# A two-layer relational graph convolution on one core: 123 single-row tiles in place of 116, spread by other steps over two DMA-issuing engines

## The chip, the cores and the metric

The kernel runs on one core of one Trainium2 chip. A core has five engines with an instruction queue each: PE (TensorE, matrix products), DVE (VectorE), ACT (ScalarE), POOL (GpSimd) and SP (SyncE). DMAs are started by SP, ACT and POOL, and the queue of an engine is worked off in order. The metric is the device time of one execution in microseconds. The profile holds one execution, with its own time.

## The reference

Two layers of a relational graph convolution over 12500 nodes with 128 features and 200000 edges of 8 relations, then a residual and a layer norm. Edges come sorted by destination. Cut to what is computed:

```python
def _rgcn_conv(x, src, dst, et, basis, comp, root, bias):
    W = jnp.einsum('rb,bio->rio', comp, basis)
    xw = jnp.einsum('ni,rio->nro', x, W)
    msgs = xw[src, et]
    seg = dst * N_REL + et
    summed = jax.ops.segment_sum(msgs, seg, num_segments=N_NODES * N_REL)
    cnt = jax.ops.segment_sum(jnp.ones(...), seg, num_segments=N_NODES * N_REL)
    mean = summed / jnp.maximum(cnt, 1.0)[:, None]
    agg = mean.reshape(N_NODES, N_REL, HIDDEN).sum(axis=1)
    return agg + x @ root + bias
...
h = x
for l in range(2):
    h = jax.nn.relu(_rgcn_conv(h, src, dst, et, basis[l], comp[l], root[l], bias[l])) + h
return _layernorm(x + h)
```

## The kernel before

The 200000 edges are 1563 tiles of 128 edges, and eight tiles make an octet: 196 octets (Q = 8, NQ = 196). Each layer is one pass over the octets. The order of the instructions on every engine is written out by hand in `ordered_path`: calls of `plan.add` record an operation with the cells it reads and writes, and `plan.emit` writes them out with the semaphore waits that follow from those cells. Nothing is scheduled by a tool, so what stands behind what in an engine's queue is the order of these calls.

*Gathers.* Per tile, POOL issues one indirect DMA that fetches 128 rows of 512 bytes (`gather`, L766): in layer 1 rows of `x`, in layer 2 rows of `y_d`, a table in DRAM of every node's features times every relation's weights, 51 MB. They land in `rows`, a ring of seven octets, and are issued five octets ahead (AHEAD = 5). The last six octets (LATE = 6, from octet 190) are different: they are issued two octets ahead in the program's order (CLOSE = 2), and each has one more wait, for the latest octet of means then in the order. So gather(190) waits until PE has done octet 187, gather(191) octet 188, and so on. The gathers of layer 2 stand behind all gathers of layer 1 in POOL's queue, and one of them (L760, with a fix-up list) waits for the whole table to have been stored.

*Single-row tiles.* For some tiles POOL issues nothing. Instead SP or ACT loads the offsets of the rows into registers (L697) and starts one DMA of 512 bytes per row (L702). `lists` names these tiles: an engine, a first tile, an end, a step, the rows that one operation fetches (a part), the lead in octets, and the places where rows land. The places are buffers that are free at that time: `jmp`, `comp_sb` and `sel` for SP in layer 1; five quarters of a `y_row` buffer, then two of `mixer`, for ACT in layer 1; the two `sT` buffers in layer 2. `lone_rows` hands the parts out in each octet: for SP all parts whose tile is within the lead, for ACT one part per octet of each list. Before, layer 1 has 32 such tiles on SP (in parts of 32 rows), and 5 and 18 on ACT (in parts of 16, eight octets for a tile); layer 2 has 31 on SP and 30 on ACT, in parts of 32. That is 55 + 61 = 116, and POOL's gathers are 1508 and 1502.

*Layer 1.* In octet o of the loop come, in this order: `gathers`; `means(o)`, PE's products of the rows with the weighted one-hots of their destinations (L1276); a batch of copies on ACT (L623: a half of the table `y_row`, the product `ys` and two halves of `sT`) with the store of a table block to `y_d` (L620), if one is complete; the parts on SP; the one-hots of octet o + 2 on DVE (L1188); the part on ACT; `product(o - 1)` on PE (L1308), which needs the `sT` that ACT copied; `place(o - 2)` (L1339); and up to two halves of a table block on PE (L1406). PE's next octet of means writes the banks that ACT's copies read. From octet 53 to octet 187 each octet has an ACT part.

*Layer 2.* In octet q come: `gathers`, the parts on SP and on ACT, `add_rows` on PE (L1451), the one-hots of octet q + 2 on DVE, and one step of a list `todo`. A finished group of eight node tiles puts ten steps on it: transposes, an addition, statistics, `aggr` (L1530), a square root on ACT (`root_of`, L1533), two empty ones, a reciprocal on DVE (`one_by`, L1537), the scaling and the store. For the last full group the transposes come at octet 178, the root at 182 and the reciprocal at 185.

The last lines of the layer 1 loop that bear on this:

```python
        means(o)
        batch(o)
        ...
        if o > 1:
            lone_rows(0, "SP", o)
        ...
        onehot(0, o + 2, o - 1)
        ...
        if o > 1:
            lone_rows(0, "ACT", o)
        ...
            product(o - 1)
```

Of the kernel before, what the change touches and what calls it, by code (L numbers as in the profile page):

```python
# [8 lines left out]
F32 = mybir.dt.float32  # L9
# [419 lines left out]
def ordered_path(  # L429
# [26 lines left out]
    P = 128  # L456
# [11 lines left out]
    Q = 8  # L468
# [29 lines left out]
    def keep(shape, dtype, name):  # L498
        return const.tile(shape, dtype, name=name)
# [16 lines left out]
    jmp = keep([P, P], I32, "jmp")  # L516
# [37 lines left out]
    comp_sb = keep([P, L * R * NB], F32, "comp_sb")  # L554
# [8 lines left out]
    mixer = keep([P, L * R, K], F32, "mixer")  # L563
# [39 lines left out]
    plan = Plan(tc, {"hw": 8, "aq": 4, "gq": 4, "sr": 8, "ar": 8})  # L603
# [35 lines left out]
    def floats(t, n):  # L639
        return t[:, n * P:(n + 1) * P]  # L640

    sT_f = [t.rearrange("p r g k -> p (r g k)") for t in sT_r.tiles]
    yr_f = yr_r.tiles[0].rearrange("p r d -> p (r d)")
    yr_cells = [("y_row", 0, 0), ("y_row", 0, 1)]
    mixer_f = mixer.rearrange("p m k -> p (m k)")
    idx_f = idx.bitcast(F32)
    lists = [
        [("SP", 90, 1552, 47, 32, 15, [(jmp.bitcast(F32), ["jmp"], []), (comp_sb, ["comp"], []),
                                     (sel.rearrange("p g k -> p (g k)"), ["sel"], [])]),
         ("ACT", 13 * Q + 2, 46 * Q, 8 * Q, 16, 10, [(floats(yr_f, j), yr_cells, yr_cells) for j in range(5)]),  # L650
         ("ACT", 53 * Q + 2, 1552, 8 * Q, 16, 10, [(floats(mixer_f, j), ["mixer"], []) for j in range(2)])],
        [("SP", 62, 1552, 49, 32, 15, [(floats(sT_f[0], j), [("sT", 0, 0), ("sT", 0, 1)], []) for j in range(4)]),
         ("ACT", 65, 1552, 50, 32, 15, [(floats(sT_f[1], j), [("sT", 1, 0), ("sT", 1, 1)], []) for j in range(4)])]]
    single, at_row = [{}, {}], [0, 0]
    for l in range(L):
        for k, (_, t0, t1, by, _, _, hosts) in enumerate(lists[l]):
            for i, t in enumerate(range(t0, t1, by)):
# [4 lines left out]
    offs = iota_f.bitcast(I32)  # L662
    byte = mybir.dt.uint8
    pending = [[[(t, j) for t in range(t0, t1, by) for j in range(P // ch)] for _, t0, t1, by, ch, _, _ in lists[l]]
               for l in range(L)]

    def lone_tile(l, t):

        k, i, _ = single[l][t]
        hosts, ch = lists[l][k][6], lists[l][k][4]  # L670
        n = i % len(hosts)
        return hosts[n][0], [("lone", l, k, n, j) for j in range(P // ch)] + hosts[n][2]
# [6 lines left out]
    def lone_rows(l, e, q):  # L679


        for k, (by, _, _, _, ch, lead, hosts) in enumerate(lists[l]):
            waiting = pending[l][k]
            while by == e and waiting and waiting[0][0] // Q - lead <= q:
                t, j = waiting.pop(0)
                _, i, r = single[l][t]
                o, cells = lone_tile(l, t)
                writes, reads = [cells[j]], [("offs", l)]
                if i < len(hosts) and j == 0:
                    writes += hosts[i][1]  # L690
                if l == 1 and i == 0 and j == 0:
                    reads += y_done
                table_b = (x if l == 0 else y_d).bitcast(byte).rearrange("n d -> (n d)")

                def emit(j=j, r=r, o=o, ch=ch, table_b=table_b):
                    eng = nc.sync if e == "SP" else nc.scalar
                    _, at = nc.values_load_multi_w_load_instructions(  # L697
                        offs[r:r + 1, l * P + j * ch:l * P + (j + 1) * ch],
                        engines=[mybir.EngineType.SP if e == "SP" else mybir.EngineType.Activation],
                        min_val=0, max_val=(N * (1 if l == 0 else R) - 1) * D * 4,  # L700
                        skip_runtime_bounds_check_because="the source of an edge is a node and its type a relation")
                    return [eng.dma_start(o[j * ch + i:j * ch + i + 1, :].bitcast(byte),  # L702
                                          table_b[bass.ds(v, 4 * D)].rearrange("(p d) -> p d", p=1))
                            for i, v in enumerate(at)]

                plan.add(e, emit, reads, writes, lane="sr" if e == "SP" else "ar", n=ch)
                if e == "ACT":
                    break

# [460 lines left out]
    dms, sT, ys, pl, ym = {}, {}, {}, {}, {}  # L1170
# [149 lines left out]
    def place(g):  # L1320

        m = tiles_of(g) * K
        t, c = pl.pop(g)
        o, oc = ys.pop(g)
        k = two_blocks(g)
        opens = g == 0 or two_blocks(g - 1) != k
        last = g == NG - 1 or two_blocks(g + 1) != k
        if opens:
            b, bc = po_b[k % 2]
            acc[k] = b.rearrange("p t d -> p (t d)")[:, :2 * P], bc  # L1330
        a, ac = acc[k]
        root_in = opens and k >= 0
        reads = [c, oc]
        if root_in:
            xt, xc = x_cols(k)
            reads += xc + [("w", 0, R)]

        def emit():
            ins = nc.tensor.matmul(a, o[:m], t[:m], start=opens, stop=last and not root_in)  # L1339
            if root_in:  # L1340
                ins = nc.tensor.matmul(a[:, :rows_of(k)], w_sb[:, 0, R, :], xt, start=False, stop=last)
            return ins

        pe(emit, reads, [ac])
        return k if last else None
# [207 lines left out]
    def sup(q):  # L1553
        return (q * Q + G) // (2 * G) - 1
# [99 lines left out]
    for o in range(NG - 3):  # L1654
# [8 lines left out]
        if o > 1:  # L1663
            lone_rows(0, "SP", o)
# [6 lines left out]
        if o > 1:  # L1671
            lone_rows(0, "ACT", o)
# [15 lines left out]
        if o > 1:  # L1688
            k = place(o - 2)
            close(k)  # L1690
            if k is not None and k % S == S // 2 and k // S + 1 < NX:
                n = k // S + 1
# [82 lines left out]
    for q in range(NQ):  # L1775
# [4 lines left out]
        k = sup(q)  # L1780
        if gathers(1, q):
            pool(lambda: nc.gpsimd.drain())
        lone_rows(1, "SP", q)
        lone_rows(1, "ACT", q)
        opens = q == 0 or sup(q - 1) != k
# [9 lines left out]
        for i in range(2):  # L1795
            for j, step in ending:
                step()
                n = j // S
# [18 lines left out]
def kernel(  # L1817
# [18 lines left out]
    flag = ctx.enter_context(tc.tile_pool(name="flag", bufs=1))  # L1836
    bad = flag.tile([1, 1], I32, name="bad")
    plan = ordered_path(tc, bad, x, src, dst, et, basis, comp, root, bias, out)
    every = [mybir.EngineType.PE, mybir.EngineType.Activation, mybir.EngineType.DVE, mybir.EngineType.Pool,
             mybir.EngineType.SP]  # L1840
# [36 lines left out]
```

## Time and profile before

| | us |
|---|---|
| median of 3 runs | 3784.03 |
| lowest and highest | 3783.49, 3790.35 |
| the profiled execution, its own time | 3783.55 |
| its span in the trace | 3781.7 |
| mean granted clock of TensorE | 0.83 |

Times in the trace count from the start of the span. Views that are used below: the page's parts (busy time of each engine, the chain of work that ended last, the costliest groups of instructions); a table of waits, with what ended an engine's idle time; stretches of the span with the busy time and the count of one line's instructions; the timeline of one engine, in which a row is a run of equal instructions, with its start, its length, and in brackets the idle time before it and its releaser. "ACTq" and "SPq" are the queues of ACT and SP when they issue DMAs; this is not counted as busy time. A tile's product in L1276 shows as two PE instructions, so an octet of means counts 16.

### The profile page before, as it was taken

The numbers are of one execution on the slowest core, as the hardware profiler recorded it, in microseconds if no ns is written. First come the engines' busy times: TensorE is split into PE (matmuls) and PEld (weight loads), VectorE is DVE, ScalarE is ACT, GpSimd is POOL, SyncE is SP. The second block draws the span as 40 slices with busy tenths as digits, with TensorE's granted clock in tenths as the row PEclk, the third lists the DMA queues.
The fourth block names the chain that finished last, engine by engine and source line by source line (L and its number), as shares of the span: only waits on it lengthen the run. The fifth ranks groups of instructions, "written<-read, shape, count | busy, mean of one in ns | idle before, by whom it ended". The sixth has DMA issues, their size and how long they took to land.

```text
span 3781.7 us, 62930 instructions
## 1 busy us (share of the span) xinstructions
PE 2413.2 (64%) x11367; PEld 1933.4 (51%) x11367; DVE 1694.7 (45%) x4752; ACT 354.0 (9%) x794; POOL 2844.7 (75%) x3019
## 2 busy tenths in 40 slices
PE   5777667777666676777765555556566555655655
PEld 3566645555555555665543444444444444444444
DVE  5556424444333333343344444444444444454444
ACT  1121211211111111111100000000000000000000
POOL 7777777777777777777777777777777777777776
PEclk8999879999888888788888787777777777787778
DMA  4122223433322222223232222222222222222222
GB/s 125 56 62 62 56 92 102 123 111 101 99 87 81 89 89 84 84 82 96 92 85 55 56 62 61 65 63 61 66 56 67 66 56 67 60 62 67 67 54 61
DMA packets 155888, 286.71 MB, mean 76 GB/s; under 512 B 67013, under 2 KB 89474, under 8 KB 155482
## 3 DMA queue, kind: packets, MB, share of 16 engines
q0 software_dynamic: 96352, 197.52, 20.3%
q10 hardware_dynamic: 30461, 55.51, 4.5%
q1 hardware_dynamic: 28669, 29.60, 3.0%
q14 instruction: 314, 2.57, 0.2%
q8 instruction: 92, 1.51, 0.2%
HBM read 223.72 MB, written 58.65 MB: 75 GB/s over the span
## 4 chain that ended last, share of the span: by engine, by line
POOL 52%; issue 19%; DMA 11%; PE 9%; ACTq 4%; ACT 2%; DVE 2%; SPq 2%; POOLq 0%; DVEq 0%
POOL rows L766 52%; DMA rows<-y_d,idy 9%; ACTq L702 3%; PE s L1276 2%; PE s L1451 1%; SPq L702 1%; ACT sT L623 1%; ACTq L697 1%; PE y L1308 1%; DVE dm L1188 1%; PE pt L1406 1%; PE ct L959 1%; PE ct L960 1%; DVE arena L949 1%; PE pt L907 1%
## 5 line engine op out<-in xcount | busy, mean ns | idle before, releaser
L766 POOL DMA_INDIRECT rows<-in_x_dram,idx x1508 | 1425.2, 945 | 462.4 <-issue 455.7
L766 POOL DMA_INDIRECT rows<-y_d,idy x1502 | 1417.4, 944 | 458.5 <-issue 446.9
L1188 DVE TENSOR_SCALAR dm<-cols,near,w 128x256 f32<-128x256 f16 x1563 | 723.8, 534 | 952.1 <-PE s L1451 570.3
L1451 PE MATMUL s<-dm,rows 128*128 128x256 f32 x1984 | 659.9, 495 | 447.7 <-DMA rows<-y_d,idy 349.0
L1451 PEld LDWEIGHTS s<-dm,rows 128*128 128x128 f32 x1984 | 491.9, 257 | 580.2 <-issue 316.9
L1188 DVE TENSOR_SCALAR dm<-cols,kr,w 128x128 f32<-128x128 f16 x1563 | 524.9, 400 | 201.8 <-PE s L1276 177.5
L1276 PEld LDWEIGHTS s<-dm,rows 128*128 128x128 f32 x3016 | 436.3, 225 | 291.7 <-DMA rows<-in_x_dram,idx 243.0
L1276 PE MATMUL s<-dm,rows 128*128 128x128 f32 x3016 | 462.1, 313 | 189.0 <-DMA rows<-in_x_dram,idx 182.3
L1451 PE MATMUL ct<-dm,rows 128*128 128x256 f32 x1014 | 341.9, 501 | 294.2 <-DMA rows<-y_d,idy 281.4
L1451 PEld LDWEIGHTS ct<-dm,rows 128*128 128x128 f32 x1014 | 255.3, 262 | 364.2 <-issue 234.5
L1308 PE MATMUL y<-w_sb,sT 128*128 128x128 f32 x1968 | 270.1, 296 | 55.8 <-ACT sT L623 55.8
L1308 PEld LDWEIGHTS y<-w_sb,sT 128*128 128x128 f32 x1968 | 257.0, 211 | 64.6 <-ACT sT L623 63.6
L1406 PE MATMUL pt<-w_sb,arena 128*128 128x512 f32 (+1 forms) x386 | 222.5, 660 | 62.3 <-DVE y_row L626 42.3
L1339 PE MATMUL po<-pl,ys 128*128 128x256 f32 x392 | 138.4, 437 | 140.8 <-ACT sT L623 135.9
L623 ACT ACTIVATE sT<-s 128x512 f32<-128x512 f32 x391 | 213.5, 606 | 83.7 <-PE s L1276 83.4
L626 DVE COPY y_row<-pt 128x512 f32<-128x512 f32 x56 | 38.7, 691 | 364.6 <-PE pt L1406 364.6
L623 ACT ACTIVATE y_row<-pt 128x512 f32<-128x512 f32 (+1 forms) x139 | 83.0, 597 | 1041.7 <-PE s L1276 574.3
L1308 PE MATMUL ct<-w_sb,sT 128*128 128x128 f32 (+1 forms) x1168 | 159.8, 296 | 0.7 <-ACT sT L623 0.7
L1308 PEld LDWEIGHTS ct<-w_sb,sT 128*128 128x128 f32 (+1 forms) x1168 | 155.0, 213 | 1.3 <-ACT sT L623 1.1
L1533 ACT ACTIVATE st<-st,eps 128x8 f32<-128x8 f32 (+1 forms) x13 | 4.0, 308 | 1586.5 <-DMA sT<-y_d 736.9
L1339 PEld LDWEIGHTS po<-pl,ys 128*128 128x128 f32 x392 | 65.2, 201 | 169.0 <-ACT sT L623 159.0
L1360 DVE TENSOR_TENSOR po<-po,carry 128x128 f32<-128x128 f32 x98 | 29.0, 296 | 263.8 <-PE s L1276 242.7
(210 smaller groups left out, 1296.9 us busy)
## 6 DMA issues: line engine op xcount, KB each, us to landing
sT<-y_d SPq DMA_DIRECT2D x3968, 0.5 KB
sT<-y_d ACTq DMA_DIRECT2D x3840, 0.5 KB
y_d<-y_row ACTq DMA_DIRECT2D x96, 512.0 KB
mixer<-in_x_dram ACTq DMA_DIRECT2D x2304, 0.5 KB
rows<-in_x_dram,idx POOLq DMA_INDIRECT x1508
rows<-y_d,idy POOLq DMA_INDIRECT x1502
jmp<-in_x_dram SPq DMA_DIRECT2D x1408, 0.5 KB
comp_sb<-in_x_dram SPq DMA_DIRECT2D x1408, 0.5 KB
```

Of the source, the lines that this page charges most:

```text
L623: act(lambda: nc.scalar.activation(out_t, in_t, AF.Copy), reads, writes)
L626: vec(lambda: nc.vector.tensor_copy(out_t, in_t), reads, writes)
L697: _, at = nc.values_load_multi_w_load_instructions(offs[r:r + 1, l * P + j * ch:l * P + (j + 1) * ch], engines=[mybir.EngineType.SP if e = ...
L702: return [eng.dma_start(o[j * ch + i:j * ch + i + 1, :].bitcast(byte), table_b[bass.ds(v, 4 * D)].rearrange("(p d) -> p d", p=1)) for i, v ...
L766: ins.append(nc.gpsimd.indirect_dma_start(out=t[:, i - q * Q, :], out_offset=None, in_=table_t, in_offset=bass.IndirectOffsetOnAxis(ap=ids ...
L907: last = nc.tensor.matmul(pt[:, b, :], t[:, b, :], m, start=(i == 0), stop=(i == len(parts) - 1))
L1188: emits.append(lambda i=i: nc.vector.tensor_scalar(t[:, i - q * Q, :wide], cols[:, :wide], ids[:, i:i + 1], w[:, i:i + 1], op0=ALU.is_equa ...
L1276: last = nc.tensor.matmul(s_b[i // 4][0][:, i % 4, :], lones[i][0] if i in lones else t[:, i, :], d[:, i, :], start=True, stop=True)
L1308: last = nc.tensor.matmul(y[:m], t[:, r, :nt, :].rearrange("p t k -> p (t k)"), w_sb[:, 0, r, :], start=(r == 0), stop=(r == R - 1))
L1339: ins = nc.tensor.matmul(a, o[:m], t[:m], start=opens, stop=last and not root_in)
L1406: pe(lambda: nc.tensor.matmul(hb[:n].rearrange("p r d -> p (r d)"), hT[:, j * P:j * P + n], w_sb[:, 1, k * H:(k + 1) * H, :].rearrange("p ...
L1451: ins = nc.tensor.matmul(a, lones[i][0] if i in lones else t[:, i, :], d[:, i, :], start=(opens and i == 0), stop=(last and i == n - 1 and ...
```

## The change

Four entries of `lists` get other steps, and the parts of ACT in layer 1 get another size.

- SP in layer 1: every 45th tile from tile 91, not every 47th from 90; 33 tiles, not 32.
- ACT in layer 1: every seventh octet, not every eighth; 5 and 21 tiles, not 5 and 18. A tile is still spread over one part an octet, so now over seven, of 18, 18, 18, 19, 18, 18 and 19 rows (`parts_of`), where it was eight parts of 16.
- SP in layer 2: every 47th tile, not every 49th; 32 tiles, not 31.
- ACT in layer 2: every 48th tile from tile 63, not every 50th from 65; 32 tiles, not 30.

Together these are 59 + 64 = 123 single-row tiles, and POOL's gathers become 1504 and 1499. In layer 1, ACT's parts stand in octets 3 to 37 and 43 to 189, where they were in 3 to 42 and 43 to 186. ACT's last tile in layer 2 becomes tile 1551, of octet 193, where it was tile 1515, of octet 189. The leads, the landing places and the order of everything else stay.

```diff
     lists = [
-        [("SP", 90, 1552, 47, 32, 15, [(jmp.bitcast(F32), ["jmp"], []), (comp_sb, ["comp"], []),
+        [("SP", 91, 1552, 45, 32, 15, [(jmp.bitcast(F32), ["jmp"], []), (comp_sb, ["comp"], []),
                                      (sel.rearrange("p g k -> p (g k)"), ["sel"], [])]),
-         ("ACT", 13 * Q + 2, 46 * Q, 8 * Q, 16, 10, [(floats(yr_f, j), yr_cells, yr_cells) for j in range(5)]),
-         ("ACT", 53 * Q + 2, 1552, 8 * Q, 16, 10, [(floats(mixer_f, j), ["mixer"], []) for j in range(2)])],
-        [("SP", 62, 1552, 49, 32, 15, [(floats(sT_f[0], j), [("sT", 0, 0), ("sT", 0, 1)], []) for j in range(4)]),
-         ("ACT", 65, 1552, 50, 32, 15, [(floats(sT_f[1], j), [("sT", 1, 0), ("sT", 1, 1)], []) for j in range(4)])]]
+         ("ACT", 13 * Q + 2, 46 * Q, 7 * Q, 18, 10, [(floats(yr_f, j), yr_cells, yr_cells) for j in range(5)]),
+         ("ACT", 53 * Q + 2, 1552, 7 * Q, 18, 10, [(floats(mixer_f, j), ["mixer"], []) for j in range(2)])],
+        [("SP", 62, 1552, 47, 32, 15, [(floats(sT_f[0], j), [("sT", 0, 0), ("sT", 0, 1)], []) for j in range(4)]),
+         ("ACT", 63, 1552, 48, 32, 15, [(floats(sT_f[1], j), [("sT", 1, 0), ("sT", 1, 1)], []) for j in range(4)])]]
...
+    def parts_of(ch):
+        k = P // ch
+        return [P * j // k for j in range(k + 1)]
...
                 o, cells = lone_tile(l, t)
+                c0, c1 = parts_of(ch)[j:j + 2]
...
-                        offs[r:r + 1, l * P + j * ch:l * P + (j + 1) * ch],
+                        offs[r:r + 1, l * P + c0:l * P + c1],
...
-                    return [eng.dma_start(o[j * ch + i:j * ch + i + 1, :].bitcast(byte),
+                    return [eng.dma_start(o[c0 + i:c0 + i + 1, :].bitcast(byte),
...
-                plan.add(e, emit, reads, writes, lane="sr" if e == "SP" else "ar", n=ch)
+                plan.add(e, emit, reads, writes, lane="sr" if e == "SP" else "ar", n=c1 - c0)
```

More of the change, by code (lines that the diff above doesn't have):

```diff
@@ L693, in lone_rows, with emit @@
                 table_b = (x if l == 0 else y_d).bitcast(byte).rearrange("n d -> (n d)")
-                def emit(j=j, r=r, o=o, ch=ch, table_b=table_b):
+                def emit(c0=c0, c1=c1, r=r, o=o, table_b=table_b):
                     eng = nc.sync if e == "SP" else nc.scalar
                     _, at = nc.values_load_multi_w_load_instructions(
-                        offs[r:r + 1, l * P + j * ch:l * P + (j + 1) * ch],
+                        offs[r:r + 1, l * P + c0:l * P + c1],
                         engines=[mybir.EngineType.SP if e == "SP" else mybir.EngineType.Activation],
```

## The prediction, made before the changed kernel ran

> **What bounds the kernel now.** I read the page's parts 1, 4 and 5 first, then the table of waits for POOL.
>
> ```profile
> span 3781.7 us, 62930 instructions
> PE 2413.2 (64%) x11367; PEld 1933.4 (51%) x11367; DVE 1694.7 (45%) x4752; ACT 354.0 (9%) x794; POOL 2844.7 (75%) x3019
> POOL 52%; issue 19%; DMA 11%; PE 9%; ACTq 4%; ACT 2%; DVE 2%; SPq 2%; POOLq 0%; DVEq 0%
> L766 POOL DMA_INDIRECT rows<-in_x_dram,idx x1508 | 1425.2, 945 | 462.4 <-issue 455.7
> L766 POOL DMA_INDIRECT rows<-y_d,idy x1502 | 1417.4, 944 | 458.5 <-issue 446.9
> POOL rows L766 <- issue: 902.6, 2957, 0.3
> ```
>
> POOL is busy for 75% of the span, yet the rest is not waiting: 902.6 us of idle time are 2957 gaps of at most 0.3 us with the releaser "issue". Busy and gap together, a gather takes (1425.2 + 462.4)/1508 = 1.252 us in layer 1 and (1417.4 + 458.5)/1502 = 1.249 us in layer 2. The 3010 gathers make 3763 of the 3782 us: POOL runs from one to the next, and every gather taken off it is worth 1.25 us as long as nothing makes it wait instead. ACT's "9%" leaves out what this change loads: instructions that issue DMAs are not counted as busy, so the timeline has to be read for ACT and SP.
>
> **What the change removes.** Single-row tiles go from 55 to 59 in layer 1 and from 61 to 64 in layer 2, so 4 and 3 gathers fewer: 4 x 1.252 + 3 x 1.249 = 8.75 us. The rows come in over SP and ACT instead, and three covers must hold.
>
> *SP in layer 1.* Two rows:
>
> ```profile
> 1004.67 49.72 SPq L702 DMA_DIRECT2D jmp<-in_x_dram  x128
> 1057.75 49.69 SPq L702 DMA_DIRECT2D comp_sb<-in_x_dram  x128
> ```
>
> One tile takes 1057.75 - 1004.67 = 53.1 us of SP. After the change an octet holds 8 - 8/45 - 8/56 = 7.68 gathers, 9.61 us of POOL (before, 8 - 8/47 - 8/64 = 7.70 and 9.64), so a tile every 45 tiles is one every 45/8 x 9.61 = 54.1 us (before, every 47: 56.6). SP keeps up with 1.0 us to spare, and its lead of 15 octets (144 us) is 91 us more than a tile takes. Cost 0; if a tile took 55 us, 33 of them would lose 30 us, still inside the lead.
>
> *ACT in layer 1.* The spare time of ACT is the first thing to go:
>
> ```profile
> 1045.94 0.60 ACT L623 ACTIVATE y_row<-pt 128x512 f32<-128x512 f32 x1 [8.48 <-issue]
> 1047.68 5.34 ACTq L702 DMA_DIRECT2D mixer<-in_x_dram  x16
> 1053.07 0.60 ACT L623 ACTIVATE y_row<-pt 128x512 f32<-128x512 f32 x1 [5.39 <-PE s L1276]
> L697 ACTq TENSOR_LOAD <-iota_f x135: 1197/2041/2632, 545.5 to 1818.3; - x135
> ```
>
> Sixteen rows take 5.34 us, 0.334 each. After the change a part has 128/7 = 18.29 rows, so 0.76 us more in each octet (bounds 0 and 0.76: nothing if ACT was waiting anyway). The load of offsets before it, 2.04 us, is paid once an octet in both. All of ACT's octet stands in one queue: batch (y_row, ys, two sT), table store, load, rows. "8.48 <-issue" says that the batch waited for nothing but the rows ahead of it. An octet without a table store takes 1053.07 - 1045.94 = 7.13 us. From octet 53 on every octet has a part; the rows of PE's means count 16 an octet:
>
> ```profile
> 541.40:627.10 85.70, 20.38 (x145) 20.44 (x145) 0.90 0.34 110
> 627.10:772.80 145.70, 35.58 (x272) 34.55 (x272) 0.96 0.37 110
> 772.80:919.10 146.30, 34.29 (x241) 33.31 (x242) 0.93 0.36 113
> 919.10:1523.40 604.30, 169.73 (x1008) 156.13 (x1008) 0.87 0.29 88
> 1523.40:1614.50 91.10, 18.81 (x129) 18.89 (x130) 0.78 0.28 84
> 1614.50:1736.00 121.50, 31.84 (x225) 31.96 (x224) 0.86 0.29 87
> 1736.00:1821.30 85.30, 25.87 (x145) 24.14 (x145) 0.90 0.31 98
> 0.00:541.40 541.40, 405.96 (x429) 0.88 0.26 74
> 0.00:1821.30 1821.30, 1373.33 (x1453) 0.88 0.29 89
> L620 ACTq DMA_DIRECT2D y_d<-y_row x9: 378/379/384, 545.1 to 624.2; - x9
> L620 ACTq DMA_DIRECT2D y_d<-y_row x15: 378/378/380, 776.7 to 915.8; - x15
> L620 ACTq DMA_DIRECT2D y_d<-y_row x33: 378/378/380, 938.1 to 1519.8; - x33
> L620 ACTq DMA_DIRECT2D y_d<-y_row x7: 378/379/380, 1625.0 to 1732.7; - x7
> L620 ACTq DMA_DIRECT2D y_d<-y_row x7: 378/378/379, 1749.7 to 1817.9; - x7
> ```
>
> The first seven rows are stretches of the means' line, the two after them POOL's gathers up to 541.4 and up to 1821.3 us, the rest the table stores in stretches 1, 3, 4, 6 and 7. They hold 9, 17, 15, 63, 8, 14 and 9 octets. Stretches 1 and 3 have a store in each octet and take (85.7 + 146.3)/24 = 9.67 us an octet, which is POOL's own 9.64. So with a store, ACT has no spare time, and 0.76 us more makes 10.43 against 9.61; without one it has 7.89.
>
> Call the time by which PE trails POOL's issue the lag. At 541.4 us POOL had issued 429 gathers, and octets 0 to 52 hold 411 (424 tiles less 13 singles): the lag is 18 x 1.25 = 22.5 us. At 1821.3 us it is (1453 - 1451) x 1.25 = 2.5: before, ACT just worked the lag off. With the change, stretch by stretch (PE's time less 9.61 an octet):
>
> - 1: 85.7 + 9 x 0.76 = 92.5 against 86.5: lag 28.5
> - 2: 145.7 + 17 x 0.76 = 158.6 against 163.4: 23.7
> - 3: 146.3 + 15 x 0.76 = 157.7 against 144.2: 37.2
> - 4: 33 x 10.43 + 30 x 7.89 = 580.9 against 605.4: 12.7
> - 5: 91.1 and half of the 8 x 0.76, since PE, not ACT, is waited for in its longest octet (the row below): 94.1 against 76.9: 29.9
> - 6: 7 x 10.43 + 7 x 7.89 = 128.2 against 134.5: 23.6
> - 7: 7 x 10.43 + 2 x 7.89 = 88.8 against 86.5: 25.9
>
> ```profile
> 1546.46 1.11 ACT L623 ACTIVATE wide<-pt 128x512 f32<-128x512 f32 x1 [16.60 <-PE s L1276]
> 1821.30 1.16 PE L1276 MATMUL s<-dm,rows 128*128 128x128 f32 x8
> 1822.52 0.83 PE L1276 MATMUL s<-dm,rows 128*128 128x128 f32 x6
> 1837.72 0.94 POOL L766 DMA_INDIRECT rows<-in_x_dram,idx  x1 [0.30 <-issue]
> 1868.95 3.78 PE L1276 MATMUL s<-dm,rows 128*128 128x128 f32 x16 [5.14 <-DMA rows<-in_x_dram,idx]
> 1912.13 0.94 POOL L760 DMA_INDIRECT jmp<-y_d,fix_i  x1 [2.31 <-DMA y_d<-y_row]
> ```
>
> Mid-layer the lag costs nothing: the ring holds seven octets and gathers run five ahead. The last six octets' gathers are let out earlier but each waits for an octet of means: gather(190) for octet 187. Before, those ended at 1822.52 + 0.83 = 1823.35, 14.4 us ahead of POOL's 1837.72. After, POOL has issued octets 0 to 187 (1447 gathers) at 1821.3 - 6 x 1.25 = 1813.8, PE begins octet 187 at 1813.8 + 25.9 = 1839.7 and ends it at 1841.8, while POOL is ready at 1837.72 - 5.0 = 1832.7: it stands for 9 us, and behind this gather stand all of layer 2's. PE then does five octets, the last two without parts, in about 37 us (between 5 x 7.13 and stretch 2's 5 x 8.57 = 43) where it took 1868.95 - 1821.30 = 47.6, waiting for rows. Its 18.4 us of delay shrink to 7.8, and from 1868.95 to the landed table at 1912 (gather's wait above) the chain is PE's and ACT's own and keeps them. Layer 1 so ends 7.8 us later, not 5.0 earlier. Bounds: with all of 0.76 hidden the lag is at most 8 and the 5.0 are gained; with store octets at stretch 3's 9.75 us and the additions whole in the last three stretches it is about 39, and the loss 21. The lag at 541.4 us I leave as it is, though 35 parts before it have grown too; what stays of them adds to the lag.
>
> *Layer 2.* Both queues issue without a pause:
>
> ```profile
> 2628.78 69.82 ACTq L702 DMA_DIRECT2D sT<-y_d  x160
> 2598.80 79.31 SPq L702 DMA_DIRECT2D sT<-y_d  x184
> L702 ACTq DMA_DIRECT2D sT<-y_d x3840: 231/233/596, 1913.8 to 3624.8; - x192
> DVE st L1537 <- ACT st L1533: 40.9, 4, 24.8
> 3709.55 5.38 PE L1451 MATMUL s<-dm,rows 128*128 128x256 f32 x16 [4.36 <-DMA rows<-y_d,idy]
> 3726.91 0.95 POOL L766 DMA_INDIRECT rows<-y_d,idy  x1 [0.30 <-issue]
> ```
>
> A tile takes ACT 69.82/160 x 128 = 55.9 us there and (3624.8 - 1913.8)/30 = 57.0 over the layer, SP 79.31/184 x 128 = 55.2. One falls due every 48/8 x 9.6 = 57.6 us on ACT (before 60) and 47/8 x 9.6 = 56.4 on SP (58.8). They keep up, but gain no reserve. In ACT's row the longest issue, 596 ns, stands beside 233 at the median: some rows wait for something. The Trainium skill (Perfetto Trace Analysis, "DMA Instruction — HWDGE (DVE, Sync)") says that the time of such an instruction can include a wait for the lock of a descriptor generator that sequencers share; no run here shows the lock itself. The trace agrees in the spread of that row; by the rule the pace would fall as both queues issue more, and the sum would be the third rival's, below; by the rows it stays at 55.9 to 57.0.
>
> ACT's last tile is now 1551 (octet 193), due after octet 181's turn, and its rows go out ahead of the last full norm's root on ACT. DVE's reciprocal waits for that root (the 24.8 us above is such a wait), the one-hots of octet 188 stand behind it on DVE, PE's octet 188 behind them, and gather(191) waits for that octet. ACT ends 32 tiles at 1913.8 + 7.8 + 32 x 56.4 = 3726 (56.4 is the mean of 55.9 and 57.0), PE is done with octet 188 some 7 us later (5.38 and the small steps), and POOL would be at gather(191) at 3726.91 + 7.8 - 3.75 = 3731: a stall of 2 us, by 55.9 none, by 57.0 about 22. I take 2.
>
> **Sum**, on the profiled execution (3783.55, 0.5 under the median 3784.03): 3783.55 + 7.8 - 3.75 + 2 = 3789.6, so 3790.
>
> **Rivals.**
>
> *ACT's rows are absorbed.* For it: the octets without a store have 2 us to spare, and PE waits for rows in part of them. Against it: stretches 1 and 3, where 24 octets in a row leave none. If the lag at octet 187 is under 13 us, nothing waits and all 8.75 us come: 3774.8.
>
> *The lag is longer.* The same mechanism past 33 us at octet 187, when the octets without a store recover less than their 2.5 us or stretch 5 takes the whole addition. At 35 layer 1 ends 16.9 us late: 3783.55 + 16.9 - 3.75 + 2 = 3799. For it: the quoted store-less octet is one of many, and others may be slower. Against: stretch 6 of before took 121.5 us, near the 7 x 9.67 + 7 x 7.13 = 117.6 of my two octets.
>
> *Layer 2's issue queues fall behind.* Past 57.6 us a tile ACT is late at every tile and at the last root; at 57.0 the stall of gather(191) is 22 us, at 56.8 about 15: 3783.55 + 7.8 - 3.75 + 15 = 3803. For it: 57.0 is the layer's own mean. Against: it holds pauses in which ACT, ahead, waited.
>
> *The change doesn't do what it says* is not open: the order of instructions has 1504 and 1499 gathers, and parts of 18, 18, 18, 19, 18, 18, 19 rows.
>
> **Chances.** Forecast (lag 18 to 33) 45%, its own range 3782 to 3797; absorbed 20%; longer lag 20%; layer 2 behind 15%. Under 0.2%, 7.6 us, a change cannot be told from none. The forecast gives 33 of its points to "same", 11 to slower, 1 to faster; absorbed 16 faster and 4 same; longer lag 20 slower; layer 2 1 same and 14 slower: faster 0.17, same 0.38, slower 0.45. The range takes in the absorbed case's 3774.8 below and both slower cases up to 3808.
>
> **What would show it.** In the new trace: POOL's table of waits with one or more waits for the means' line of several us each, about 9 in all, near 1833 us; gathers issued by PE's octet 187 about 20 more than octets 0 to 187 hold; ACT's batches released by "issue" in nearly all store octets; the gather of the fixes at about 1920 us; the L1537 row with many more waits. If octet 187 starts at once behind its rows, ACT's step is wrong, and the gain is whole; if POOL's wait stands at the end of layer 2 instead, ACT's pace there is.

## The result, and the profile after

The changed kernel takes 4168.85 us (median of 5 runs, 4153.34 to 4170.39) against 3783.49 us for the kernel before beside it (5 runs): a ratio of 1.1011, 95% interval 1.1000 to 1.1023. It is 385 us slower, where 3790 and at most 3808 us were forecast. Beside some runs of the next section, those named e, f, g and k, the kernel before took about 5780 us instead of 3784, with register moves on SP and ACT of up to 1.4 us (run f6) that take 0.03 in the trace of before, so of those runs little more than durations of single loads is read. The page of the changed kernel, its lines that answer to those shown of before (the line numbers have moved by five: L771 is the gather, L1281 the means of layer 1, L1456 the matrix products of layer 2, L702 the load of offsets, L707 the rows), with the chain by lines of the kernel before as the last row:

```profile
span 4151.5 us, 64735 instructions
PE 2481.9 (60%) x11367; PEld 1973.5 (48%) x11367; DVE 1692.5 (41%) x4752; ACT 351.6 (8%) x794; POOL 2836.8 (68%) x3012
ACTq 30%; POOL 26%; issue 20%; DMA 9%; ACT 7%; PE 7%; DVE 2%; POOLq 0%; DVEq 0%; SPq 0%
POOL rows L771 26%; ACTq L707 20%; ACTq L702 9%; DMA rows<-y_d,idy 9%; ACT sT L623 4%; ACT y_row L623 2%; PE s L1281 1%; PE y L1313 1%; PE s L1456 1%; ACTq L620 1%; DVE dm L1193 1%; ACT ys L623 1%; PE pt L912 1%; PE po L1344 0%; PE pt L1411 0%
L771 POOL DMA_INDIRECT rows<-in_x_dram,idx x1504 | 1420.0, 944 | 834.0 <-issue 423.6
L771 POOL DMA_INDIRECT rows<-y_d,idy x1499 | 1414.7, 944 | 459.1 <-issue 446.8
...
POOL rows L766 52%; DMA rows<-y_d,idy 9%; ACTq L702 3%; PE s L1276 2%; PE s L1451 1%; SPq L702 1%; ACT sT L623 1%; ACTq L697 1%; PE y L1308 1%; DVE dm L1188 1%; PE pt L1406 1%; PE ct L959 1%; PE ct L960 1%; DVE arena L949 1%; PE pt L907 1%
```

The chain that ended last has changed hands: before, ACT's queue had 4% of it and POOL 52%, now ACT's queue has 30%. Its two main parts are the rows (L707, 20%, where they had 3% as L702) and the load of offsets (L702, 9%, where it had 1% as L697). POOL's gathers of layer 1 have the same busy time for each, and 834.0 us of idle time where they had 462.4. The table of POOL's waits in the changed kernel (total, times, longest) and two rows of its timeline name them, and a row for PE's means from octet 52 to the start of octet 187 (start, end and length first):

```profile
POOL rows L771 <- issue: 870.5, 2852, 0.3
POOL rows L771 <- PE s L1281: 407.0, 112, 51.7
POOL jmp L765 <- DMA y_d<-y_row: 7.1, 1, 7.1
...
2192.43 0.94 POOL L771 DMA_INDIRECT rows<-in_x_dram,idx  x1 [51.67 <-PE s L1281]
2283.41 0.94 POOL L765 DMA_INDIRECT jmp<-y_d,fix_i  x1 [7.12 <-DMA y_d<-y_row]
...
597.70:2190.20 1592.50, 336.99 (x2160) 345.83 (x2160) 0.79 0.26 76
```

All of the loss lies in layer 1. The gather of the fix-ups, behind the stored table, starts at 2283.41 where it started at 1912.13, 371.3 us later. From there to the end of the span it is 4151.5 - 2283.41 = 1868.1 us, where it was 3781.7 - 1912.13 = 1869.6: layer 2 gained 1.5 us. POOL waits 407 us for the means of layer 1, 112 times: not only at the end, as forecast, but throughout. 341.4 us of it lie ahead of the gather of octet 190, the first of more than 0.6 us at 220 us. By the program's order a gather there can wait for the means only when the ring of seven octets is full, so PE had fallen that far behind. PE begins octet 52 at 597.7 us, where it began it at 541.4, 56.3 us late, and from there to octet 187 it takes 1592.5/135 = 11.80 us an octet, where it took 1279.9/135 = 9.48 and POOL needs 9.61.

What made ACT slow shows in its timeline. Six rows of the changed kernel in the middle of layer 1:

```profile
1210.40 0.60 ACT L623 ACTIVATE y_row<-pt 128x512 f32<-128x512 f32 x1 [9.41 <-issue]
...
1212.18 0.38 ACTq L620 DMA_DIRECT2D y_d<-y_row  x1
1217.58 6.03 ACTq L707 DMA_DIRECT2D mixer<-in_x_dram  x18
1223.71 0.60 ACT L623 ACTIVATE y_row<-pt 128x512 f32<-128x512 f32 x1 [11.56 <-issue]
...
1227.99 5.99 ACTq L707 DMA_DIRECT2D mixer<-in_x_dram  x18
1234.03 0.60 ACT L623 ACTIVATE y_row<-pt 128x512 f32<-128x512 f32 x1 [8.57 <-issue]
```

The octet with a table store takes 1223.71 - 1210.40 = 13.31 us, the one without 10.32; the prediction had 10.43 and 7.89. The rows cost what was forecast, 6.0 us for 18. But between the end of the store's issue at 1212.56 and the first row at 1217.58 lie 5.0 us, and in the next octet the rows begin 4.3 us behind the first copy. There stands the load of offsets, which the timeline doesn't list, and which the view of its line shows. Rows of that line (duration in ns: least, median, longest; first and last start): ACT's in octets 48 to 189 of layer 1, then one at a time, two of the changed kernel and one of before:

```profile
L702 ACTq TENSOR_LOAD <-iota_f x142: 1647/4420/5518, 556.6 to 2223.2; - x142
L702 ACTq TENSOR_LOAD <-iota_f x1: 4093/4093/4093, 1223.8 to 1223.8; - x1
L702 ACTq TENSOR_LOAD <-iota_f x1: 1670/1670/1670, 1248.3 to 1248.3; - x1
...
L697 ACTq TENSOR_LOAD <-iota_f x1: 1198/1198/1198, 1025.0 to 1025.0; - x1
```

The median load takes 4.42 us where it took 2.04. And it has two values: the two single loads of 18 offsets, both beside the same copies, take 4.09 and 1.67 us. Sorted by the place where the load begins in the list of offsets, the loads that begin beside ACT's copies (behind a table store each kind takes about 0.9 us more):

```
kernel    first offset  offsets  median us
before    0, 16, .. 112    16       1.20
changed        0           18       1.69
changed       36           18       1.68
changed       18           18       4.10
changed       54           19       4.31
changed       73           18       4.19
changed       91           18       4.18
changed      109           19       4.32
```

Two of seven parts begin at a multiple of four offsets, 16 bytes, and these are fast. The theory from here: a load that begins at such a place takes a step of some 0.24 us for each four offsets and one for each that is left over at its end (18 take 0.48 us more than 16), and one that begins elsewhere takes some 0.21 us for each offset. The seven loads take 24.5/7 = 3.49 us on the mean, 2.29 more than before, and the rows of an octet 0.76 more.

### The profile page after: what moved, and what is told of

Read it like the earlier page. It is cut to its first block, busy times and chain, and to the rows that moved or that the text cites. A ratio compares the mean times of both kernels' runs of the same rounds, so it can differ in the third digit from the quotient of the medians.

```text
span 4151.5 us, 64735 instructions
## 1 busy us (share of the span) xinstructions
PE 2481.9 (60%) x11367; PEld 1973.5 (48%) x11367; DVE 1692.5 (41%) x4752; ACT 351.6 (8%) x794; POOL 2836.8 (68%) x3012
## 4 chain that ended last, share of the span: by engine, by line
ACTq 30%; POOL 26%; issue 20%; DMA 9%; ACT 7%; PE 7%; DVE 2%; POOLq 0%; DVEq 0%; SPq 0%
POOL rows L771 26%; ACTq L707 20%; ACTq L702 9%; DMA rows<-y_d,idy 9%; ACT sT L623 4%; ACT y_row L623 2%; PE s L1281 1%; PE y L1313 1%; PE s L1456 1%; ACTq L620 1%; DVE dm L1193 1%; ACT ys L623 1%; PE pt L912 1%; PE po L1344 0%; PE pt L1411 0%
## 5 line engine op out<-in xcount | busy, mean ns | idle before, releaser
L771 POOL DMA_INDIRECT rows<-in_x_dram,idx x1504 | 1420.0, 944 | 834.0 <-issue 423.6
L771 POOL DMA_INDIRECT rows<-y_d,idy x1499 | 1414.7, 944 | 459.1 <-issue 446.8
L1456 PE MATMUL s<-dm,rows 128*128 128x256 f32 x1984 | 628.4, 478 | 447.9 <-DMA rows<-y_d,idy 332.4
L1456 PEld LDWEIGHTS s<-dm,rows 128*128 128x128 f32 x1984 | 472.8, 248 | 573.8 <-issue 291.3
L1456 PE MATMUL ct<-dm,rows 128*128 128x256 f32 x1008 | 339.4, 500 | 315.7 <-DMA rows<-y_d,idy 192.2
L1281 PEld LDWEIGHTS s<-dm,rows 128*128 128x128 f32 x3008 | 453.9, 229 | 104.1 <-issue 99.8
L1344 PE MATMUL po<-pl,ys 128*128 128x256 f32 x392 | 171.4, 528 | 547.9 <-ACT sT L623 544.3
L1281 PE MATMUL s<-dm,rows 128*128 128x128 f32 x3008 | 452.7, 310 | 0.7 <-ACT sT L623 0.7
L1456 PEld LDWEIGHTS ct<-dm,rows 128*128 128x128 f32 x1008 | 253.0, 261 | 385.0 <-issue 220.9
L1313 PE MATMUL y<-w_sb,sT 128*128 128x128 f32 x1968 | 286.9, 307 | 111.6 <-ACT sT L623 111.6
L1344 PEld LDWEIGHTS po<-pl,ys 128*128 128x128 f32 x392 | 76.5, 236 | 580.6 <-ACT sT L623 570.7
L1313 PEld LDWEIGHTS y<-w_sb,sT 128*128 128x128 f32 x1968 | 271.7, 221 | 120.0 <-ACT sT L623 119.6
L1411 PE MATMUL pt<-w_sb,arena 128*128 128x512 f32 (+1 forms) x386 | 295.8, 860 | 45.3 <-DVE y_row L626 43.9
L1313 PE MATMUL ct<-w_sb,sT 128*128 128x128 f32 (+1 forms) x1168 | 147.8, 281 | 0.7 <-ACT sT L623 0.7
L1411 PEld LDWEIGHTS pt<-w_sb,arena 128*128 128x128 f32 (+1 forms) x386 | 87.7, 259 | 125.2 <-DVE y_row L626 113.0
L1313 PEld LDWEIGHTS ct<-w_sb,sT 128*128 128x128 f32 (+1 forms) x1168 | 141.4, 197 | 1.3 <-ACT sT L623 1.1
```

The costliest lines, as they stand in the source:

```text
L771: ins.append(nc.gpsimd.indirect_dma_start(out=t[:, i - q * Q, :], out_offset=None, in_=table_t, in_offset=bass.IndirectOffsetOnAxis(ap=ids ...
L1281: last = nc.tensor.matmul(s_b[i // 4][0][:, i % 4, :], lones[i][0] if i in lones else t[:, i, :], d[:, i, :], start=True, stop=True)
L1313: last = nc.tensor.matmul(y[:m], t[:, r, :nt, :].rearrange("p t k -> p (t k)"), w_sb[:, 0, r, :], start=(r == 0), stop=(r == R - 1))
L1411: pe(lambda: nc.tensor.matmul(hb[:n].rearrange("p r d -> p (r d)"), hT[:, j * P:j * P + n], w_sb[:, 1, k * H:(k + 1) * H, :].rearrange("p ...
L1456: ins = nc.tensor.matmul(a, lones[i][0] if i in lones else t[:, i, :], d[:, i, :], start=(opens and i == 0), stop=(last and i == n - 1 and ...
```

## The experiments

The rivals to tell apart: that loads off a multiple of four make the loss (alignment), that any load of more than 16 offsets is slow (length), and that the rows beyond 16 overload ACT by themselves (rows, the prediction's mechanism at a larger size).

The times that decide are those of the runs h and m, beside which the kernel before took 3782 and 3786 us.

**e1, f1 and h1: aligned loads, the same rows.** The load begins at the multiple of four below the part and ends at the one above it:

```diff
-                        offs[r:r + 1, l * P + c0:l * P + c1],
+                        offs[r:r + 1, l * P + c0 // 4 * 4:l * P + -(-c1 // 4) * 4],
...
-                            for i, v in enumerate(at)]
+                            for i, v in enumerate(at[c0 % 4:c0 % 4 + c1 - c0])]
```

> The changed kernel, in which each load of offsets begins at a multiple of four offsets and holds a multiple of four (20 or 24); the rows fetched by each part stay 18 or 19. Theory (a load that begins off a multiple of four offsets takes one step for each offset, about 0.2 us, where an aligned one takes a step for four): ACT's loads in layer 1 fall from a median of 4.1 us to 1.4 to 1.7 us behind a copy, POOL's waits for the means of layer 1 from 407 us to 10 to 30 us, and the time comes to that of the prediction, 3775 to 3810 us. Rival (rows beyond 16 in a part overload ACT by themselves): the loads may get shorter but layer 1 stays long, about 4150 us. Rival (more than 16 offsets make a load slow, wherever it begins): loads of 4 us and more, 4150 us or above.

> The same kernel as e1, once more, since in that call every kernel, the one before too, took over 5700 us, for stalls in SP's and ACT's rows that all of them share. Against a kernel before of about 3784 us: theory (alignment of the loads) 3775 to 3810 us, with loads of 1.45 to 1.7 us behind a copy and 10 to 30 us of POOL waiting for the means of layer 1; rival (rows beyond 16 in a part) about 4150 us.

> The changed kernel with loads of offsets that begin at a multiple of four (as e1 and f1). Against a kernel before of about 3784 us: theory (alignment) 3775 to 3810 us; rival (the rows beyond 16 of a part) about 4150 us. Where the kernel before takes over 5700 us again: theory, less than the changed kernel in the same call by 60 us or more; rival, the same as the changed kernel within 0.5%.

**h2: the changed kernel itself, beside h1.**

> The changed kernel itself, beside the one with aligned loads. Against a kernel before of about 3784 us: 4150 to 4170 us, as it was. Where the kernel before takes over 5700 us again: theory (alignment), 60 us or more above h1; rival (rows beyond 16, or layer 2), the same as h1 within 0.5%.

e1 and f1 took 5924 and 5923 us beside 5785 and 5786 for the kernel before, which tells nothing of the rivals; the loads were short already, 1.46 us for 20 offsets and 1.70 for 24 beside copies. h1 took 3841.58 us (4 runs) and h2 4161.88 beside 3781.83 for the kernel before: ratios of 1.0156 (1.0139 to 1.0173) and 1.1010 (1.0991 to 1.1028). With aligned loads and not one row less, 320 of 380 us are gone. The rival "rows" is out as the main cause. But h1 is also 32 us above the upper end that the theory's expectation gave it: something of 60 us is left, and POOL's waits for the means are 62.6 us, where e1's expectation had 10 to 30. Rows of h1: its loads from octet 52 to 187, POOL's waits, and the gather behind the longest wait:

```profile
L702 ACTq TENSOR_LOAD <-iota_f x135: 1433/2342/2890, 545.4 to 1884.3; - x135
POOL rows L771 <- PE s L1281: 62.6, 12, 45.2
...
1892.37 0.94 POOL L771 DMA_INDIRECT rows<-in_x_dram,idx  x1 [45.17 <-PE s L1281]
```

The wait that the prediction described is there, at the first gather of octet 190, for the means of octet 187: 45.2 us, not 9. Where the time went shows in the means' line of h1, in the seven stretches of the prediction, cut at the same octets:

```profile
539.30:635.40 96.10, 21.76 (x145) 22.04 (x145) 0.86 0.36 105
635.40:795.20 159.80, 40.93 (x272) 41.31 (x273) 0.88 0.38 105
795.20:958.50 163.30, 38.89 (x241) 39.57 (x241) 0.82 0.36 107
958.50:1563.80 605.30, 153.47 (x1008) 156.65 (x1009) 0.82 0.31 88
1563.80:1660.90 97.10, 17.45 (x128) 17.63 (x128) 0.77 0.29 81
1660.90:1792.70 131.80, 32.69 (x224) 33.42 (x224) 0.83 0.29 81
1792.70:1889.00 96.30, 20.77 (x144) 21.20 (x144) 0.85 0.23 73
```

The second column is the length. The prediction's stretches were 92.5, 158.6, 157.7, 580.9, 94.1, 128.2 and 88.8, together 1300.8 us; here they are 1349.7, so 48.9 more. An aligned load of 20 or 24 offsets takes (5 x 1.46 + 2 x 1.70)/7 = 1.53 us, 0.33 more than the 1.20 of 16, and 135 octets x 0.33 = 44.6 us. So by this estimate nearly all of what is left over the prediction is the same term, at its smaller size: even aligned, a load grows with the offsets that it brings. No run took this rest away by itself.

**e2 and f2: parts cut at multiples of four.**

```diff
-        return [P * j // k for j in range(k + 1)]
+        return [-(-P * j // k) // 4 * 4 for j in range(k + 1)]
```

> The changed kernel with the seven parts cut at multiples of four: 16, 20, 16, 20, 20, 16 and 20 rows, each load as long as its part. Theory (alignment to four offsets): loads of 1.2 us for 16 and about 1.45 us for 20, and 3775 to 3810 us, as in the run with padded loads or a few us less, since no offset is loaded in vain. Rival (rows beyond 16): about 4150 us. Rival (length, not alignment): loads of 20 take 4.3 us, four of seven parts, and the time is 3900 to 4000 us.

> The same kernel as e2, once more: parts of 16, 20, 16, 20, 20, 16 and 20 rows. Theory (alignment): 3775 to 3810 us and within 6 us of f1, since the rows are the same in sum and the loads 0.1 to 0.2 us shorter on the mean. Rival (rows beyond 16): about 4150 us.

5936 and 5928 us beside 5785 and 5786, which decides nothing. The loads of e2 took 1.22 us for 16 offsets and 1.46 for 20 beside copies, with no offset loaded in vain. "Length" is out with this: 20 offsets take a third of what 18 take at a bad place. The table above has it already: 18 offsets from place 36 take 1.68 us. How many us these parts save against h1 where the kernel before takes 3784 us was not tried.

**e3, f3, k3 and m3: the old parts, shifted.** The kernel before, with parts cut at 0, 18, 34 and so on to 114 and 128. No row is added and no gather removed:

```diff
+                c0, c1 = j * ch, j * ch + ch
+                if ch == 16:
+                    c0, c1 = c0 + 2 * (j > 0), min(c1 + 2, P)
...
-                        offs[r:r + 1, l * P + j * ch:l * P + (j + 1) * ch],
+                        offs[r:r + 1, l * P + c0:l * P + c1],
```

> The kernel before, with its parts of ACT in layer 1 still eight to a tile, cut at 0, 18, 34, 50, 66, 82, 98, 114 and 128: no row more, no gather fewer, but seven of eight loads begin off a multiple of four. Theory (alignment): those loads of 16 take 3.6 to 3.8 us behind a copy where they took 1.2, ACT's octet grows by about 2.2 us and layer 1 by 200 to 280 us: 3980 to 4070 us. Rival (rows, or length over 16): no change, 3784 us within 0.3%, up to 3800 us.

> The same kernel as e3, once more. Its loads took 3.67 us at the median behind a copy for 16 offsets in that run, 1.2 when aligned, so the load's part of the theory is settled; what is open is what it costs. Theory (the load alone makes most of the loss): 3980 to 4070 us, POOL waiting 150 to 300 us for the means of layer 1. Rival (the loss needs the rows as well): up to 3850 us.

> The kernel before with its parts of 16 shifted by two offsets (as e3 and f3), where the kernel before takes about 3784 us. Seven of eight loads begin off a multiple of four; no row more, no gather fewer. Theory (alignment alone makes most of the loss): h2 less h1 gave 320 us for loads longer by 1.96 us on the mean; here they are longer by 2.17 us, with 0.76 us less of rows, so 3784 + 200 to 300 us: 3980 to 4080 us. Rival (the load costs much only on top of the rows): up to 3850 us.

> As k3: the kernel before with its parts of 16 shifted by two offsets. Where the kernel before takes about 3784 us: theory (the loads alone make most of the loss) 3980 to 4080 us; rival (they cost much only on top of the rows) up to 3850 us. Where it takes over 5700 us: the same as the kernel before within 0.5%, as in f3 and k3, since SP ends the chain there.

e3, f3 and k3 took 5769, 5774 and 5772 us beside 5785, 5786 and 5784, the rival's number as it stands, though SP's queue had 57% of the chain that ended last in e3 and 48% in k3 (ACT's 1% and 9%), so that a loss of ACT's could hide behind it. m3 is the one to read: 4005.96 us (4 runs) beside 3785.91, a ratio of 1.0581 (1.0565 to 1.0598), inside the theory's 3980 to 4080 and far from the rival's 3850. ACT's loads in layer 1 and POOL's waits in m3:

```profile
L700 ACTq TENSOR_LOAD <-iota_f x152: 1652/3765/5215, 401.0 to 2053.0; - x152
POOL rows L769 <- PE s L1279: 244.5, 73, 55.5
```

Sixteen offsets now take 3.66 us beside a copy, fourteen 3.25 and the eighteen from place 0 1.66. The loss of 220 us comes with no change but the place at which the loads begin.

**e4: layer 2 alone**, its two entries of `lists` changed in the kernel before.

> The kernel before with the two entries of layer 2 alone changed (SP every 47th, ACT every 48th from 63). Theory of the prediction for layer 2 (3 gathers fewer at 1.25 us, and up to 2 us of stall at its end): 3780.3 to 3782.3 us, 1.7 to 3.7 us less than before. Rival (the two queues fall behind): gather(191) waits 15 us or more, 3795 us or above.

5843 us beside 5785, which decides nothing; m6 stands in for it.

**f6, k6 and m6: all but ACT's part of layer 1.** The kernel before with SP's entry of layer 1 and both entries of layer 2:

```diff
-        [("SP", 90, 1552, 47, 32, 15, ...
+        [("SP", 91, 1552, 45, 32, 15, ...
...
-        [("SP", 62, 1552, 49, 32, 15, ...
-         ("ACT", 65, 1552, 50, 32, 15, ...
+        [("SP", 62, 1552, 47, 32, 15, ...
+         ("ACT", 63, 1552, 48, 32, 15, ...
```

> The kernel before with SP's entry of layer 1 (every 45th from 91) and both entries of layer 2 changed, and ACT in layer 1 left at eight parts of 16: 120 single-row tiles, 4 gathers fewer. Theory (each gather is worth 1.25 us where nothing waits, and SP and layer 2 hold): 3784 less 1.25 and less 1.75 to 3.75, 3779 to 3781 us. Rival (SP or layer 2 fall behind): 3790 us or above.

> As f6: SP's entry of layer 1 and both of layer 2 changed, ACT in layer 1 as before, 4 gathers fewer. Theory: 3779 to 3782 us, faster than the kernel before by 2 to 5 us. Rival (SP at one tile every 54 us, or layer 2's queues, fall behind): 3786 us or above.

> As k6: SP's entry of layer 1 and both of layer 2 changed, ACT in layer 1 as before, 4 gathers fewer. Where the kernel before takes about 3784 us: theory 3779 to 3782 us, 2 to 5 us below it; rival (SP or layer 2 fall behind) 3786 us or above. Where it takes over 5700 us: about 125 us above it, as in f6 and k6, which says nothing of either.

f6 and k6 took 5914 and 5912 us beside 5786 and 5784. A row of SP's timeline in k6 shows what bounds there, in layer 2:

```profile
3000.05 199.56 SPq L702 DMA_DIRECT2D sT<-y_d  x286
```

A row with its share of the loads costs 0.70 us, where it cost 79.31/184 = 0.43 in the trace of before. In m6 it is 3779.96 us (11 runs) beside 3785.91 (15 runs), a ratio of 0.9986 (0.9977 to 0.9995): 6 us faster, where 2 to 5 were expected, and 0.14% is less than the 0.2% under which the prediction calls a change none, though the interval leaves out 1. Rows of m6: POOL's waits, the gather of the fix-ups, and ACT's rows of layer 2:

```profile
POOL rows L766 <- issue: 899.6, 2947, 0.3
POOL rows L766 <- PE s L1451: 5.0, 11, 1.9
...
1908.69 0.94 POOL L760 DMA_INDIRECT jmp<-y_d,fix_i  x1 [0.90 <-issue]
...
L702 ACTq DMA_DIRECT2D sT<-y_d x4096: 231/234/638, 1910.2 to 3704.4; - x196
```

The means hold POOL nowhere in layer 1 (its longest wait for them is 0.3 us), and PE waits for none of SP's rows. ACT works through its 32 tiles of layer 2 in (3704.4 - 1910.2)/32 = 56.1 us each, and the longest wait of a gather for the means of layer 2 is 1.9 us. This version is the fastest of those that were run.

**g0 to g3: ACT's tiles of layer 1 and no other.** Made to take SP out of the way: SP has no single-row tiles in either layer and ACT none in layer 2 (empty ranges in `lists`); g0 has ACT's parts of before, g1 those of the changed kernel, g2 those with h1's loads, g3 those shifted as in m3.

> The kernel before with no single-row tiles but ACT's 23 in layer 1 (parts of 16): SP has none in either layer, ACT none in layer 2, and POOL issues these 93 tiles instead. It is the base for g1, g2 and g3, made so that the stalls of SP's rows in the runs e and f, where SP ended the chain, can't cover what ACT does. Where POOL runs through: 3784 + 93 x 1.25 = 3900 us, if ACT alone issues its rows without the stalls. If ACT's rows stall as well, 3950 us or more.

> As g0, with ACT's 26 tiles of the changed kernel in layer 1 (seven parts of 18 or 19, loads as they fall). Theory (the loads that begin off a multiple of four offsets, with the rows): layer 1 ends as late as in the changed kernel, about 2284 us, so 2284 + 1868 + 64 x 1.25 = 4230 us, 300 to 350 us above g0. Rival (the loss came from SP or from layer 2): 3896 us.

> As g1, with loads that begin at a multiple of four offsets; the rows are the same. Theory (alignment): most of the loss of g1 goes; rows 0.76 us and loads 0.3 us more in an octet leave the lag of the prediction and its wait at the end of layer 1: 3895 to 3925 us. Rival (the rows beyond 16): within 60 us of g1, 4170 to 4230 us.

> As g0, parts of 18, six times 16, and 14, seven of eight loads off a multiple of four; no row more than in g0. Theory (alignment alone makes most of the loss): ACT's octet grows by 2.2 us, 11.8 us with a table store and 9.3 without against POOL's 9.84: 4040 to 4130 us. Rival (it needs the rows): 3900 to 3920 us.

4713, 4851, 4770 and 4886 us, beside 5780 for the kernel before. g0's 3900 was missed by 800 us: the stalls are not SP's alone, and the four can't be held against the sizes expected. Against g0 the changed parts cost 138 us (300 to 350 expected) and the loads off their place with no row added 173 (140 to 230 expected), so g3 came out above g1, where the theory has it at least 100 us below: these runs bear out neither the sizes nor the order. g2's four runs lie between 4684 and 4783, too far apart for a number.

## Why the prediction was wrong

*The bound and the worth of a gather: right.* A gather is worth 1.25 us where nothing else waits: m6 removed four, 5.0 us by the prediction's price, and gained 6, with an interval of 2 to 9.

*SP in layer 1: right.* Every 45th tile fits: in m6 PE waited for none of SP's rows, and no gather of layer 1 waited over 0.3 us for the means.

*Layer 2: close, in part by luck.* Forecast: 3.75 us gained by three gathers, 2 us lost to the stall of gather(191), 1.75 net. From the fix-ups' gather to the end the changed kernel gained 1.5 us, m6, with the same entries, 3.5, and h1 lost 0.4. The tight place is there: ACT's last rows end just ahead of the root at 4078.62 us, and DVE's reciprocal waits 7.45 us for it. But ACT's pace, put at 56.4 us a tile, is 56.1 in m6, and at that pace the prediction's own sum has no stall; the changed kernel has one of 1.48 us at gather(190) and one of 0.68 at gather(191). That these two come from the root is not shown.

*ACT in layer 1: the mechanism right, one term mis-sized, and with it the result.* PE did fall behind POOL because ACT's queue left no spare time, and the gather of octet 190 did wait for the means of octet 187. The step that failed is this sentence: "The load of offsets before it, 2.04 us, is paid once an octet in both." The term was carried over at its old size, and 2.04 us was the median of two kinds, 1.20 beside copies and some 2.15 behind a table store. Beside copies it measured 3.49 us against 1.20, 2.29 us more in an octet, three times the 0.76 us of rows that the prediction counted. The trace of before had only loads of 16 and 32 offsets, all at multiples of 16, so no row of it showed the slow kind. With an octet so much longer, two more sentences failed: "Mid-layer the lag costs nothing" (341.4 us of POOL's waits came there), and the lag at 541.4 us that was left as it is (56.3 us were lost ahead of octet 52; in h1, with short loads, none). But the diff showed that the loads would begin at 18, 36, 54, 73, 91 and 109, and a size that the trace does not show needs a bound on both sides, which the load did not get. Its two sizes in the rows of before, 1.20 us for 16 offsets beside copies and some 2.2 for 32, hinted that it grows with its length (by 0.06 us an offset, 0.25 for four more). By the estimate above that growth is most of what separates h1 (3841.58) from the forecast (3790): with 48.9 us more in the seven stretches, 3789.6 + 48.9 = 3838.5 us.

*The range: wrong for the same reason.* Its upper end came from variations of the lag at 0.76 us an octet; none of the rivals touched the load.

*What was said to show it.* A wait near 1833 us of about 9 us: it came at 2192 and lasted 51.7. Some 20 gathers ahead at octet 187: 16, and it can't be more, since gather(190), the 17th, waits for that octet. Batches of ACT released by "issue" in nearly all octets with a store: in 68 of 89 from octet 52 on, and 21 more by the landing of ACT's own rows. Fix-ups at about 1920 us: 2283. Many more waits of DVE's reciprocal for the root: 13 of 257.4 us in sum, where there were 4 of 40.9.

*Stays open:* what makes the load slow off a multiple of four. The runs show the place and the size, not the mechanism.

## What to carry to other kernels

When a change resizes or moves a transfer, the small instruction ahead of it (here a load into registers) is resized and moved too, so price it at its new size and place, and give it a range where the trace has no such row. Where a list is loaded into registers as here, begin and end each load at a multiple of four entries: from such a place 18 took 1.68 us and 20 took 1.46. When an engine has no spare time in its octet, a third of a microsecond there, paid 135 times, costs more than the seven gathers saved: put the extra work where a queue runs ahead, as SP's and layer 2's did in m6.

## What the runs showed of the hardware

*Loads into registers.* The loads read a list that lies in a buffer of the kernel. Beside a copy, one that begins at a multiple of four entries took 1.20 us for 16 entries, 1.46 for 20 and 1.70 for 24, so 0.24 to 0.26 us for four; in layer 2, behind rows, 32 took about 2.2. For 18 entries it took 1.68, more than for 20: the two left over cost a step each. Off a multiple of four entries it took 3.25 us for 14, 3.66 for 16, 4.1 to 4.2 for 18 and 4.3 for 19: 0.21 us for one. The Trainium skill (Runtime: NRT & Kernel Launch, "Instruction fetch mechanics") gives about 200 ns for each register, even in bulk, for the loads into registers that the runtime puts in. For loads off their place the trace agrees (0.21 us); for aligned ones the measurement decides, and it is 0.06 us a register.

*Copies run beside loads and rows on ACT, and the load is paid for in full.* In the kernel before the load of 1.20 us at 1025.0 us begins 0.1 us behind the first of four copies; the rows begin at 1026.29, as soon as it is done, while the last copy runs to 1026.64. In the changed kernel the load at 1223.8 takes 4.09 us, and the rows begin at 1227.99. What the load takes longer, the rows begin later, and the copies cover none of it. Behind a table store every load is about 0.9 us longer: in the changed kernel 5.0 us stood between a store and its rows.
